# Layer 1: three regrouping transfers issued with the first mixings, a quarter of layer 0's projections added earlier, and the last group norm's small products placed two steps on

## The chip, the cores and the metric

The kernel runs on one core of a Trainium2 chip. The time is device time in microseconds of one execution; the figure before is the median of three runs. The trace is that of one profiled execution.

## The reference

Two attention layers act on x of shape (8, 512, 32, 32), each as x + layer(group_norm(x)); T = 1024 tokens, C = 512, 8 heads of 64. All is float32.

```
# layer 0
q, k, v = split(qkv_w @ norm(x))
a   = softmax(q^T k * scale) applied to v
x   = x + proj_w @ (norm(x) + a) + proj_b
# layer 1
attn = (q^T k) * scale                        # per head h
attn = einsum('gh,bhqT->bgqT', w_head, attn)  # the heads are mixed
attn = softmax(attn)
attn = (attn - mean) / sqrt(var + EPS) * gamma + beta   # over a whole head
x    = x + w_proj @ (attn @ v) + b_proj
```

## The kernel before, in words

Everything is unrolled, and the order of the instructions on each engine is the order in which the Python code issues them (a manual schedule). An Agenda is a list of functions with a slot each; `ag.run(slot)` issues those that are due, within a slot in the order in which they were added. All the transfers that this text speaks of are issued from the SP queue, but for a few small ones on POOL's. [...]

**Layer 0.** For each image the projections k, v, q and output are computed by `project0` as seven products of half-size blocks instead of eight. A result has four quarters (i, j). TensorE runs product 1, product 2 (into the same two banks of PSUM as product 1), and then products 6, 5, 7, product 3 (`banks5, left[:, 6]`, which adds to product 5's banks), and last product 4, whose two banks come from the pair tagged `a0`. VectorE adds up: `u2` from product 1 and product 6, `u3` from `u2` and product 7. `finish(i, j, x, y)` writes a quarter: for q and k two additions of 128x512 (L958), for v one of 128x1024 (L980), for the output (`out0`) one addition of 128x1024 and two of 128x512 with a store to DRAM each (L1051, L1057, L1060). Quarter (1,1) needs only `s5`, ScalarE's copy of product 5, and `u3`. The next projection's product 1 takes the `a0` banks that quarter (1,0) frees.

**Layer 1.** For each image an `Attention1` object is stepped through half-steps x = 0 to 36. Half-step x computes the scores of block x in two halves (`scores`, L1656), copies them to `raw` (L1669 on VectorE, L1671 on ScalarE), and, with a lag of MLAG = 4, mixes the heads of block y = x - 4 (`mix`, L1704), takes the exponential (L1710), and one half-step later multiplies by v (`values`, L1750). Two blocks make a step t. When the last scores of an odd x are issued, eight transfers become due for its step: each moves every eighth row of `raw` into a part of `re` (L1680, 256 KB), so that a row of `re` holds the heads side by side for the mixing. `R_ORDER` = (0, 4, 1, 5, 2, 6, 3, 7) is the order of issue and of use. `raw` has two buffers, so step t + 2 writes over step t.

When they are issued is set in three places. In the lag's first half-steps, at the end of `half_step`, `self.regroup(n=NR)` issues all that are due (NR = 8). From then on each `mix` and each `values` ends with `self.regroup(last)`, which issues one that waits for the last matmul of the call. Also, once x is above 4, each `scores` issues one piece of the next image's input (`y`, 128 KB, L1356) that waits for its own last matmul.

In the first half-steps of an image the remaining products of v (`v_pair`, L1475) fill TensorE, at slots 1 and 3. In image 0 the group norm of the eighth image's layer-0 output is also computed there, in three stages from `group_stages`: `means` (a product with `gavg`, L622, behind a VectorE copy gs_m), `squares` (four small VectorE operations and a product, L633) and `end` (some twenty small VectorE operations). `v_sums` (L1492) at slot 3 needs what `end` writes. Their products take PSUM tiles from the three buffers that scores and mixings use.

Of the kernel before, what the change touches and what calls it, by code (L numbers as in the profile page):

```python
# [467 lines left out]
def tile_two_attention_layers(  # L468
# [20 lines left out]
    B, C, T = x_d.shape  # L489
# [8 lines left out]
    NR = 8  # L498
# [198 lines left out]
    with ExitStack() as l0:  # L697
# [12 lines left out]
        def score_psum(nm):  # L710
            return ps_s.tile([P, 2, FB], F32, tag="s", name=nm)
# [174 lines left out]
        def product(banks, left, right, first, by_token):  # L886


            for i in range(2):
                for h in range(2):  # L890
                    for k in range(2):
                        if by_token:
                            out = banks[i][:, h * HC : (h + 1) * HC]
                            st, mv = right[:, k, ts(2 * i + h, P)], left[:, k]
                            start = first and k == 0 and h == 0
                        elif h == 0:
                            out = banks[i]
                            st, mv = left[:, k, ts(i, P)], right[:, k]
                            start = first and k == 0
                        else:  # L900
                            continue
                        nc.tensor.matmul(  # L902
                            out, st, mv, start=start, stop=(k == 1), skip_group_check=True
                        )

        def project0(nm, which, n, finish, by_token=False):


            left = left_t[which]
            b11, b12, b21, b22 = (n[:, 2 * i : 2 * i + 2, ts(j, FB)] for i in (0, 1) for j in (0, 1))  # L910
            s1, u2, s5 = tmp[4], tmp[5], tmp[6]

            def single(name):
                return [
                    ps_a.tile([P, FB], F32, tag="a0", name=f"{nm}_{name}_{i}", bufs=2)
                    for i in range(2)
                ]

            def double(name):
                t = score_psum(f"{nm}_{name}")  # L920
                return t, [t[:, 0], t[:, 1]]

            x = single("p1")
            product(x, left[:, 0], b11, True, by_token)
            for i in range(2):
                nc.scalar.copy(s1[:, i], x[i])
            product(x, left[:, 1], b21, False, by_token)
            finish(0, 0, x, None)
            t6, banks = double("p6")
            product(banks, left[:, 4], tmp[1], True, by_token)  # L930
            nc.vector.tensor_add(u2, s1, t6)
            t5, banks5 = double("p5")
            product(banks5, left[:, 3], tmp[0], True, by_token)
            nc.scalar.copy(s5, t5)
            t7, banks = double("p7")
            product(banks, left[:, 5], tmp[2], True, by_token)
            u3 = s1
            nc.vector.tensor_add(u3, u2, t7)
            product(banks5, left[:, 6], b22, False, by_token)
            finish(0, 1, t5, u2)  # L940
            finish(1, 1, s5, u3)
            x = single("p4")
            product(x, left[:, 2], tmp[3], True, by_token)
            finish(1, 0, x, u3)
# [256 lines left out]
        for b in range(B):  # L1201
            more = b + 1 < B
            ag = Agenda()
# [61 lines left out]
    with ExitStack() as l1:  # L1265
# [14 lines left out]
        NX = 2 * NQB * NKB  # L1280
        QLAG = NX // NQB
        R_ORDER = (0, 4, 1, 5, 2, 6, 3, 7)
        MLAG = 4
# [67 lines left out]
        def y_piece(b, i):  # L1351

            if i == 0:
                y_t[b] = shared.tile([P, NCC, T], F32, tag="n", name=f"y_{b}")
            c, r = i // 4, i % 4 * 32
            return nc.sync.dma_start(  # L1356
                out=y_t[b][r : r + 32, c], in_=x1_d[b][c * P + r : c * P + r + 32, :]
            )
# [103 lines left out]
        def k_leave():  # L1462
            for fn in due:
                fn()
            due.clear()
# [173 lines left out]
        class Attention1:  # L1639
# [237 lines left out]
            def half_step(self, x, ag):  # L1877
                y, w = x - MLAG, x - MLAG - 1
                if 0 <= w < NX:
                    self.squares(w, 0)  # L1880
                    self.sum_e(w, 0)
                if x < NX:
                    self.scores(x, 0)
                if 0 <= w < NX:
                    self.squares(w, 1)
                    self.sum_e(w, 1)
                if x < NX + MLAG:
                    k_leave()
                if 0 <= w < NX:
                    self.sum_e2(w, 0)  # L1890
                    self.sum_e2(w, 1)
                k_leave()
                if 0 <= y < NX:
                    self.mix(y, 0)
                if 0 <= w < NX:
                    self.values(w, 0)
                if x < NX:
                    self.scores(x, 1)
                if 0 <= y < NX:
                    self.mix(y, 1)  # L1900
                if x <= MLAG or x >= NX:
                    self.regroup(n=NR)
                if x >= NX:
                    self.piece(n=len(self.pieces))
                ag.run(x - 0.5)
                if 0 <= w < NX:
                    self.values(w, 1)
                    self.e.pop(w)
                    if w % QLAG == QLAG - 1:
                        qb = w // QLAG  # L1910
                        self.leave(qb)
                        self.totals(qb)
                        if qb < NQB - 1:
                            ag.at(x + 2, lambda: self.reciprocals(qb, ag, x + 2))
                            ag.at(x + 6, lambda: self.divide(qb))
                ag.run(x)
# [9 lines left out]
        for b in range(B):  # L1926
            more = b + 1 < B
            a = Attention1(b)
            ag = Agenda()
            if b == 0:  # L1930
                for x, fn in zip((0, 1, 3), group_stages(B - 1, B, small_psum1)):
                    ag.at(x, fn)
            for i in range(NV):
                ag.at(1 + 2 * i, lambda i=i: v_pair(b, NV + i))
            if b == 0:
                ag.at(3, v_sums)
            free = (NX // 2 - 2 + b) % 2
            if more:
                a.pieces += [lambda i=i: y_piece(b + 1, i) for i in range(4 * NCC)]
                a.pieces += [lambda i=i: left_piece(("k", b + 1), i) for i in range(14)]  # L1940
                for c in range(NCC):
                    ag.at(24 + c, lambda c=c: normalize1(b + 1, c))

                def k_begin():
                    kp.append(k_projection(b + 1))
                    kp[0].products(1)
                    kp[0].leave(1)

                def k_go(*ms):
                    for m in ms:  # L1950
                        kp[0].products(m)
                        due.append(lambda m=m: kp[0].leave(m))

                kp = []
                ag.at(NX - 0.5, lambda: right_tile(b + 1))
                ag.at(NX - 0.5, k_begin)
                ag.at(NX, lambda: right_y(b + 1, [0, 1]))
                ag.at(NX, lambda: k_go(2))
                ag.at(NX + 1, lambda: right_y(b + 1, [2, 3]))
                ag.at(NX + 1, lambda: k_go(6, 7))  # L1960
                ag.at(NX + 1, lambda: load_w(("v", b + 1), wvT, re_t[:, free, : NCC * C]))
                ag.at(NX + 1, lambda: left_p(b))
                ag.at(NX + 2, lambda: k_go(5, 4))
                ag.at(NX + 3, lambda: k_go(3))
            else:
                a.pieces += [lambda i=i: p_piece(i) for i in range(2 * NCC)]
            for x in range(NX + MLAG + 1):
                a.half_step(x, ag)
            if not more:
                ag.flush()  # L1970
                out1_last(a)
                continue
            a.reciprocals(NQB - 1)
            a.instance()
            ag.flush()
            v_pair(b + 1, 0)
            a.instance_end()
            a.divide(NQB - 1)
            for g in range(H):
                a.affine(g)  # L1980
            right_o = re_t[:, 1 - free].rearrange("p (i k t) -> p i k t", i=4, k=2)
            combine_right(right_o, out_view(b))
            op = out1(b, right_o)
            load_left(("q", b + 1))
            v_pair(b + 1, 1)
            load_wv_again(b + 1)
            op.run()
            q_projection(b + 1).run()
# [70 lines left out]
```

## Time and profile before

| | |
|---|---|
| median of 3 runs | 4238.78 us (4232.57 to 4243.62) |
| profiled execution | 4230.7 us |
| its span, first to last instruction | 4228.9 us |
| TensorE busy | 4152.5 us, 98% |
| VectorE, ScalarE busy | 68%, 55% |
| regrouping transfers | 1024 of 256 KB |
| mean clock of TensorE | 0.997 of full |

Layer 0 fills the span up to 1805 us, layer 1 the rest, with some 306 us an image. A line of a waits view gives the engine and what it was to run, what it waited for, and the total, the number and the longest of the waits. A line of the chain gives start, length and what ran; the chain is followed back from the last instruction, so time on it is time of the kernel. "issue" is time in which the engine waited for nothing that the profile shows. In a table of windows each engine's busy time is followed by its number of instructions, and the row ends with the granted clock, the share of time that the DMA engines were busy, and the GB/s that they moved.

### The profile page before, as it was taken

To read this page: it belongs to the slowest core of one execution; us is meant where nothing else is said; L and a number is where in the kernel's file an instruction comes from. 1 tells how busy PE (TensorE), PEld (TensorE's weight loads), DVE (VectorE), ACT (ScalarE), POOL (GpSimd) and SP (SyncE) were. 2 spreads that over 40 slices of the span, in tenths; PEclk is the share of its full clock that TensorE was granted. 3 is DMA by queue.
4 is the path that set the end of the run, shared out by engine and by line. 5 is a ranking of instruction groups with operands and counts; after the bars stand their busy time and mean duration, and the time that the engine had idled before them with its cause. 6 is when DMAs were issued, how large, how long until landed. Compare 5 with 4: busy or idle time off the path is not lost.

```text
span 4228.9 us, 131405 instructions
## 1 busy us (share of the span) xinstructions
PE 4152.5 (98%) x58572; PEld 2215.3 (52%) x58572; DVE 2861.2 (68%) x3779; ACT 2319.1 (55%) x2735; POOL 60.3 (1%) x86
## 2 busy tenths in 40 slices
PE   8999999999999999999999999999999999999998
PEld 4353535353535353456466466466466466466565
DVE  4748484848484747558668668568578588588587
ACT  2717171727272726259368278278277287286386
POOL 0000000000000000000000000000000000000000
PEclk9999999999999999999999999999999999999999
DMA  3212121212121212167467377277377376485575
GB/s 130 99 61 98 55 104 48 84 45 86 45 84 48 84 48 84 58 157 196 133 168 191 118 187 191 106 199 189 104 197 187 111 200 166 125 208 146 149 180 139
DMA packets 257905, 529.35 MB, mean 125 GB/s; under 512 B 52336, under 2 KB 59888, under 8 KB 250672
## 3 DMA queue, kind: packets, MB, share of 16 engines
q1 hardware_dynamic: 254752, 520.15, 43.1%
q8 instruction: 461, 7.55, 0.7%
q0 software_dynamic: 2576, 0.69, 0.4%
q14 instruction: 116, 0.95, 0.1%
HBM read 204.50 MB, written 46.92 MB: 59 GB/s over the span
## 4 chain that ended last, share of the span: by engine, by line
PE 92%; DVE 3%; DMA 2%; ACT 1%; issue 1%; SPq 0%; DVEq 0%; ACTq 0%
PE a L1750 12%; PE m L1704 11%; PE s L1656 11%; PE s L1082 10%; PE a L1108 10%; PE pv_p L902 5%; PE pp_p L902 5%; PE pk_p L902 5%; PE pq_p L902 4%; PE pk L1400 4%; PE pq L1400 4%; PE pv L1475 4%; PE pp L1400 3%; DMA re<-raw 1%; PE t L1781 1%
## 5 line engine op out<-in xcount | busy, mean ns | idle before, releaser
L1704 PEld LDWEIGHTS m<-wmix,re 64*64 64x64 f32 x32768 | 582.1, 135 | 120.7 <-issue 55.0
L1087 ACT ACTIVATE e<-s 128x1024 f32<-128x1024 f32 x512 | 497.2, 1026 | 234.4 <-PE s L1082 232.3
L1704 PE MATMUL m<-wmix,re 64*64 64x64 f32 x32768 | 592.2, 219 | 24.5 <-issue 17.7
L1710 ACT ACTIVATE e<-m 128x1024 f32<-128x1024 f32 x512 | 525.9, 1027 | 146.1 <-PE m L1704 142.6
L1728 DVE TENSOR_TENSOR z<-z,e 128x1024 f32<-128x1024 f32 x448 | 537.7, 1218 | 76.4 <-ACT e L1710 76.2
L1732 DVE TENSOR_TENSOR z<-z,e 128x1024 f32<-128x1024 f32 x448 | 534.1, 1219 | 62.1 <-ACT e L1721 60.4
L1750 PE MATMUL a<-e,v 128*64 128x256 f32 x4096 | 559.2, 393 | 3.1 <-issue 2.5
L1656 PE MATMUL s<-k,q 64*64 64x256 f32 x8192 | 553.6, 389 | 6.7 <-DVE q L1512 2.6
L1095 DVE TENSOR_TENSOR zacc<-zacc,e 128x1024 f32<-128x1024 f32 x384 | 468.6, 1220 | 82.6 <-ACT e L1087 61.0
L1671 ACT COPY raw<-s 128x1024 f32<-128x1024 f32 x368 | 372.9, 1013 | 267.9 <-PE s L1656 230.9
L1082 PE MATMUL s<-q,k 64*64 64x512 f32 x4096 | 490.1, 593 | 2.3 <-ACT e L1087 2.3
L1108 PE MATMUL a<-e,v 64*64 64x512 f32 x4096 | 484.1, 589 | 0.0
L1721 ACT ACTIVATE e<-e 128x1024 f32<-128x1024 f32 x448 | 460.0, 1056 | 0.0
L1656 PEld LDWEIGHTS s<-k,q 64*64 64x64 f32 x8192 | 268.3, 132 | 271.7 <-issue 167.5
L1750 PEld LDWEIGHTS a<-e,v 128*64 128x64 f32 x4096 | 251.4, 136 | 125.6 <-issue 17.3
L1108 PEld LDWEIGHTS a<-e,v 64*64 64x64 f32 x4096 | 156.7, 133 | 282.8 <-issue 282.5
L1082 PEld LDWEIGHTS s<-q,k 64*64 64x64 f32 x4096 | 147.9, 133 | 275.2 <-issue 241.4
L1669 DVE COPY raw<-s 128x1024 f32<-128x1024 f32 x144 | 175.9, 1221 | 97.4 <-PE s L1656 89.0
L1475 PE MATMUL pv<-wv,y 128*128 128x512 f32 x256 | 116.3, 608 | 0.3 <-DVE raw L1669 0.3
L1480 DVE COPY v<-pv 128x512 f32<-128x512 f32 x30 | 20.7, 689 | 139.3 <-ACT v L1479 139.3
L902 PE MATMUL pv_p<-left_v,tmp 128*128 128x256 f32 x512 | 113.1, 379 | 0.0
L902 PE MATMUL pq_p<-tmp,left_q 128*128 128x512 f32 x256 | 112.5, 592 | 0.0
(316 smaller groups left out, 4128.3 us busy)
## 6 DMA issues: line engine op xcount, KB each, us to landing
re<-raw SPq DMA_DIRECT2D x1024, 256.0 KB
rzb<-zd SPq DMA_DIRECT2D x256, 128.0 KB
left_q<-left_q SPq DMA_DIRECT2D x17, 1792.0 KB
left_p<-left_p SPq DMA_DIRECT2D x17, 1792.0 KB
left_k<-left_k SPq DMA_DIRECT2D x10, 1792.0 KB
x<-in_x_dram SPq DMA_DIRECT2D x32, 512.0 KB
x<-x SPq DMA_DIRECT2D x64, 256.0 KB
left_v<-left_v SPq DMA_DIRECT2D x8, 1792.0 KB
```

Of the source, the lines that this page charges most:

```text
L902: nc.tensor.matmul(out, st, mv, start=start, stop=(k == 1), skip_group_check=True)
L1082: nc.tensor.matmul(ps[c * D : c * D + D, m], k[r, hp, k0 : k0 + D], q[r, hp, ts(f, FB)], start=True, stop=True,)
L1087: nc.scalar.activation(e[i], ps, AF.Exp, scale=S0 * S0)
L1095: nc.vector.tensor_add(zacc[g], zacc[g], e[i])
L1108: nc.tensor.matmul(acc[g][a][m * D : m * D + D], v[rows, kc, ts(2 * hp + m, D)], e[i][rows, m], start=(kc == 0), stop=(kc == NG - 1),)
L1400: nc.tensor.matmul(self.ps[m][:, i], w[:, left, k * HC + i * P : k * HC + i * P + P], right[:, k], start=(k == 0 and m != 2), stop=(k == 1 ...
L1656: last = nc.tensor.matmul(pv[c * D : c * D + D, m, j], qo_t[b][r, 2 * qb + j, hp, ts(c, D)], k_t[b][r, hp, ts(kb, KB)], start=True, stop=True,
L1704: last = nc.tensor.matmul(ps[c * D : c * D + D, a, ts(r, D)], self.re[t, r][rows, j, k0 : k0 + D], wmix[rows].rearrange("p g i -> p (g i)" ...
L1710: nc.scalar.activation(self.e[y][:, j], ps.rearrange("p a c -> p (a c)"), AF.Exp)
L1728: nc.vector.tensor_add(self.z[:, j], self.z[:, j], self.e[y][:, j])
L1732: nc.vector.tensor_add(self.z2[:, j], self.z2[:, j], self.e2[j])
L1750: last = nc.tensor.matmul(self.acc[w][two * D : two * D + D, s].rearrange("p (c i) -> p c i", i=Q8), v_t[b][:, kc, ts(g, D)], e[:, g], sta ...
```

## The change

There are three edits. In `project0` the quarter (1,1) is finished right after `u3`, ahead of product 3, where before it was finished after quarter (0,1). In `half_step` the call at the end of x = 3 issues five of its eight transfers, and the call at x = 4 is gone; the three that are left are issued one by one by the calls in `mix`. In image 0 of layer 1, `means` moves from slot 0 to slot 1 and `squares` from slot 1 to slot 2, `means` behind `v_pair`; `end` stays first in slot 3.

```
@@ project0
             nc.vector.tensor_add(u3, u2, t7)
+            finish(1, 1, s5, u3)
             product(banks5, left[:, 6], b22, False, by_token)
             finish(0, 1, t5, u2)
-            finish(1, 1, s5, u3)
             x = single("p4")
@@ half_step
-                if x <= MLAG or x >= NX:
-                    self.regroup(n=NR)
+                if x < MLAG or x >= NX:
+
+                    self.regroup(n=NR if x != MLAG - 1 else 5)
@@ the loop over images of layer 1
+            stages = group_stages(B - 1, B, small_psum1) if b == 0 else ()
             if b == 0:
-                for x, fn in zip((0, 1, 3), group_stages(B - 1, B, small_psum1)):
-                    ag.at(x, fn)
+                ag.at(3, stages[2])
             for i in range(NV):
                 ag.at(1 + 2 * i, lambda i=i: v_pair(b, NV + i))
             if b == 0:
+                ag.at(1, stages[0])
+                ag.at(2, stages[1])
                 ag.at(3, v_sums)
```

## The prediction

> **What bounds the kernel now.** I read the page first: TensorE is busy 98% of the span, so the time can fall only where TensorE idles or runs at a reduced clock. Of the 76 us of idle time, some 20 lie ahead of its first projection and 10 after its last output product. What is left is small pieces, so the next views are the list of who TensorE waited for in layer 1 (first fence; columns: us in total, times, longest) and the chain that ended last, stretch by stretch.
>
> ```profile
> PE m L1704 <- issue: 17.1, 23, 2.5
> PE m L1704 <- DMA re<-raw: 4.4, 8, 1.6
> PE s L1656 <- issue: 2.2, 1, 2.2
> ```
>
> The largest line waits for nothing that the profile names ("issue"): 17 us. In the chain the longest of these stand at one place of an image, just after its first mixing. In image 1:
>
> ```profile
> 2148.22 0.87 PE s L1656 x16
> 2149.08 0.57 PE m L1704 x37
> 2149.65 1.21 issue
> 2150.86 0.68 PE m L1704 x27
> ```
>
> Images 1 to 6 lose 1.21, 2.45, 1.11, 2.24, 0.91 and 1.50 us there, images 0 and 7 none. What TensorE lacks is instructions. Counting its instructions in order, nearly every longer "issue" gap of layer 1 sits at one position modulo 256, and ends 1.3 to 1.6 us after a packet of the instruction queue q8 lands. The DMA view says when that packet could run: ahead of image 2's stall, over 8.0 us, the data queue alone fills the engines and no instruction packet appears; it comes in the next stretch.
>
> ```profile
> q1 hardware_dynamic: 1103, 2.03, 104.3%
> re<-raw SPq DMA_DIRECT2D x6, 256.0 KB
> ...
> q1 hardware_dynamic: 36, 0.05, 14.1%
> q8 instruction: 1, 0.02, 5.3%
> ```
>
> (The first two lines are 2448.5 to 2456.5, the last two 2456.5 to 2458.) That queue holds the eight regrouping transfers of step 1, issued together when x = 3 ends. Two of the stalls cost more than their length: the stretches right after them run at half clock (last but two value of a row):
>
> ```profile
> 1811.30:1818.10 6.80, 6.14 (x24) 2.61 (x17) 1.68 (x5) 1.01 (x1) 0.00 (x0) 0.50 0.47 118
> 2459.80:2463.20 3.40, 3.40 (x80) 3.15 (x74) 1.82 (x2) 3.15 (x4) 0.00 (x0) 0.50 0.14 43
> 3077.60:3081.00 3.40, 3.40 (x70) 2.27 (x61) 2.43 (x3) 1.02 (x1) 0.00 (x0) 0.50 0.18 43
> ```
>
> The first row follows the wait of the last group norm, the other two the 2.45 and 2.24 us stalls; stalls of 1.6 us and less have no such stretch.
>
> [...]
>
> **The change, part by part.**
>
> *Regrouping.* At x = 3 five transfers go out in place of eight; the other three follow mix(0,0), mix(0,1) and mix(1,0), one each, by the regroup call that mix already makes. The count stays 1024. In image 1 the eight move from about 2139.4 to 2148.0, 1.04 us each, so five drain 3.1 us earlier, near 2145. The relief is bounded by when the block is asked for. Once TensorE enters the block before, an undisturbed fetch of layer 1 begins some 0.8 us later (0.6 to 1.2 are common); the six begin 1.8, 2.5, 1.3, 2.5, 1.0 and 2.3 us later. The gains are 1.0, 1.7, 0.5, 1.7, 0.2 and 1.5 us; images 3 and 5 ask so late (24.5 to 24.8 us after their first score) that the first deferred transfer, released at 24.0, can be in the way, so I count nothing for them: 5.9 us. The two stalls above 2.2 us fall below 1, so their half-clock stretches go: 2 x 3.41 x 0.5 = 3.4 us. Part sum **9.3 us**; bounds: all six stalls and both stretches, 12.8, and below nothing, as the second rival shows. On the SP queue the three wait for the end of a mixing, with two y pieces and step 2's transfers behind them; those wait for later matmuls anyway, and the engines carry little from 2149 to 2154 (DMA share 0.11). The last one's reader, the end of mix(2,0), comes 6.2 us after its release; the buffer for raw of step 3 is wanted at the same time.
>
> *The quarter.* VectorE now adds quarter (1,1) while TensorE is in product 3, not after quarter (0,1), so it reaches the last quarter, whose banks the next product needs, earlier. Worked on the chain at 500:
>
> ```profile
> 497.47 0.02 DVEq L958
> 497.49 0.04 issue
> 497.54 3.40 DVE q L958 x5
> 500.94 0.04 issue
> 500.98 3.27 PE pp_p L902 x7
> ```
>
> Product 4 starts at 497.26 and has eight matmuls 0.43 apart, so the next could start at 500.70: 0.28 us lost, at seven q-to-output hand-overs 2.0 us. The k-to-v hand-over of the first image loses 0.29 the same way. In the seven later ones a 0.64 us sum of exponentials stands between and the wait is for the second bank, which ends with product 4 itself: nothing. v to q shows no gap. Once, at 1735, the permuted q of layer 1 has six additions of 1.0 us and k starts at 1741.85; with the (1,1) pair done by 1735.6 the last addition starts when its bank is ready at 1739.2 and k at 1740.3: 1.55 us. Part sum **3.8 us**, 3 to 4.5. The moved quarter costs nothing where product 3 covers it: 2.4 to 3.3 us with the addition before, against 3.43; the output's is 3.9, so quarter (0,1) starts 0.4 us later there, and its bank is still free 1.6 us before a score wants it. The stores of the output change order on SP and leave earlier.
>
> *Last group norm, once.* Before, TensorE stands 2.36 us for gs_m and 0.66 for gs_sq (the rows pm L622 and pv L633 in the waits) and v_pair's product starts at 1813.65. After, scores of x = 1 follow at once, one waiting some 0.9 us for ScalarE's raw copy, and that product starts near 1810.1: 3.55 us gained. But gs_m now stands behind v_pair's copy on VectorE (0.59 + 0.69 us and hand-overs), so TensorE waits about 1.5 us for pm, then 1.3 for gs_sq behind a 1.23 us raw copy; the next v_pair starts 7.3 us after the first one's end instead of 5.1: 2.2 lost. Net 1.35. The 6.83 us at half clock go or stay (0 to 3.4); I take half, 1.7. Part sum **3.0 us**, bounds -2 (both new waits trigger half clock) and 5.
>
> The sum is 9.3 + 3.8 + 3.0 = 16.1 us. The profiled execution took 4230.7 us (span 4228.9 and 1.8 around it), so it would take 4214.6; the median of the runs shown is 8.1 us above it, and taken from that the forecast is **4222.7 us**, 0.38% faster.
>
> **Rivals.** *The fetch isn't freed.* The block may be asked for late, not held back, since the late starts are 1 to 2.5 us [...]. Then only 3.8 + 3.0 remain: 4232.0. For it: images 3 and 5. Against it: in all six images the packet starts 25.5 to 25.8 us after the first score, though their block boundaries differ by 1.8 us; what they share is the moment that the data queue drains.
>
> *The deferred transfer is late (slower).* In the chain a regrouping transfer takes 4.78 to 6.66 us from release to use. The last deferred one has 6.2. If it queues behind the two before it and the y piece and takes 8.5, mix(2,0) stands 2.3 us and the clock halves for 1.7 more: 4.0 x 8 images = 32 us, less the 16.1: 4254.7. It is slower by 0.3% from about 8.1 us on. Against it: the steady steps release their last transfer 5 us ahead with fuller engines and mostly lose under 1 us.
>
> That the change doesn't do what it says is excluded: the instruction order on SP shows the three transfers among the y pieces.
>
> **How the numbers follow.** A difference under 0.3% (12.7 us) can't be told from none. The main case has 0.70: its spread of 10 to 24 us puts 0.55 above the bound and 0.15 within. The first rival has 0.20 (0.03 faster, 0.17 same), the second 0.10 (0.08 slower, 0.02 same). Faster 0.58, same 0.34, slower 0.08. The range reaches from all stalls and both first and last clocks gained (22 us) with the 5 us by which runs scatter on one side, to the second rival's beginning on the other: 4210 to 4238.
>
> **What the profile after would show.** Right: the first 30 us of images 1, 2, 4 and 6 without an issue gap over 1 us, no half-clock stretch near 2460 and 3078, an instruction packet 23 to 25 us after the first score; product 4 followed at once by the output projection; pm and gs_sq waits of 1 to 1.5 us. Wrong: issue gaps as long as before, or a row of m waiting for re<-raw at the third mixing of each image.

## The result, and the profile after

| | before | after |
|---|---|---|
| median, first timing (5 runs each) | 4239.43 us (4232.57 to 4243.62) | 4217.70 us (4217.51 to 4219.02) |
| ratio, first timing | | 0.995 (0.9939 to 0.9962) |
| median, second timing (30 and 5 runs) | 4231.94 us (4225.59 to 4239.96) | 4217.72 us (4214.50 to 4223.78) |
| ratio, second timing | | 0.9967 (0.9954 to 0.9980) |
| profiled execution, span | 4228.9 us | 4215.8 us |
| TensorE busy, idle | 4152.5, 76.4 us | 4147.3, 68.5 us |

The kernel became faster, by 0.3 to 0.5%: 21.7 us in the first timing, 14.2 us when it was timed again. The difference between the two is all in the kernel before (4239 and 4232 us); the changed kernel has 4217.7 both times. The spans of the two profiled executions differ by 13.1 us: 7.9 us less idle time of TensorE and 5.2 us less busy time. Before, 20.5 us in five stretches ran at half clock, after 3.4 us in one (without a stretch at the very end, 6.5 and 7.2 us).

Who TensorE waited for in layer 1, after:

```profile
PE m L1704 <- issue: 14.0, 28, 1.1
PE m L1704 <- DMA re<-raw: 5.7, 10, 1.3
PE a L1750 <- issue: 1.0, 4, 0.3
```

The total of "issue" before mixings fell only from 17.1 to 14.0 us, but the longest from 2.5 to 1.1; the line of scores with its single 2.2 us wait is gone, and that before the products with v fell from 2.5 to 1.0. The chain shows the place that matters, image 2 after its first mixing. Before:

```profile
2455.99 0.91 PE m L1704 x59
2456.90 2.45 issue
2459.35 0.28 PE m L1704 x3
```

After, scores and mixings follow each other there:

```profile
2447.12 1.02 PE s L1656 x16
2448.15 0.93 PE m L1704 x64
2449.08 0.87 PE s L1656 x16
2449.95 0.96 PE m L1704 x64
```

The DMA view of the same image, first 2440.5 to 2447.5, then 2448 to 2450:

```profile
re<-raw SPq DMA_DIRECT2D x5, 256.0 KB
...
q8 instruction: 1, 0.02, 3.0%
...
re<-raw SPq DMA_DIRECT2D x1, 256.0 KB
```

Five transfers instead of eight, and the instruction packet has the engines almost to itself: no line of q1 in the second stretch (beside q8's 3.0% there is one packet of q14, 1.7%), though the first deferred transfer is issued there. The packet starts 23.2 us after the image's first score, where it was 25.5.

Granted clock (last but two value of a row) in the counterparts of the three half-clock stretches of before, with the one stretch that is left in image 0 as the second row (it stands right behind the 128 small products of `v_sums`; more on that below):

```profile
1805.00:1811.80 6.80, 6.80 (x24) 2.96 (x16) 0.79 (x1) 1.01 (x1) 0.00 (x0) 1.00 0.61 153
1831.50:1834.90 3.40, 3.40 (x84) 2.75 (x80) 0.00 (x0) 1.55 (x2) 0.00 (x0) 0.51 0.03 5
2453.00:2456.40 3.40, 3.40 (x96) 2.31 (x92) 1.87 (x3) 3.40 (x4) 0.00 (x0) 1.00 0.65 183
3066.00:3069.40 3.40, 3.40 (x94) 2.26 (x90) 1.75 (x2) 3.06 (x4) 0.00 (x0) 1.00 0.57 157
```

The quarter's move, in the chain at the hand-over from q to output, where 3.40 us of VectorE stood between the products:

```profile
491.83 7.72 PE pq_p L902 x18
499.55 3.86 PE pp_p L902 x9
```

VectorE is off the chain there. At the hand-over from q to k of layer 1 two additions ended the wait before:

```profile
1739.75 2.06 DVE q L1018 x2
1741.81 0.04 issue
1741.85 3.27 PE pk_p L902 x7
```

After, one is left:

```profile
1735.87 1.09 DVE q L1018
1736.96 0.04 issue
1737.00 5.42 PE pk_p L902 x12
```

The waits of TensorE in the first part of image 0, before (1800 to 1830 us):

```profile
PE pm L622 <- DVE gs_m L620: 2.4, 1, 2.4
...
PE pv L633 <- DVE gs_sq L631: 0.7, 1, 0.7
```

After (1795 to 1850 us):

```profile
PE pm L622 <- DVE gs_m L620: 1.6, 1, 1.6
...
PE pv L633 <- DVE gs_sq L631: 1.2, 1, 1.2
PE s L1656 <- ACT raw L1671: 0.9, 1, 0.9
...
```

The three of after are the waits that the prediction named for the new order (about 1.5, 1.3 and 0.9 us).

### The profile page after: what moved, and what is told of

Same layout as the page of the kernel before. It is cut to its first block, busy times and chain, and to the rows that moved or that the text cites. A ratio compares the mean times of both kernels' runs of the same rounds, so it can differ in the third digit from the quotient of the medians.

```text
span 4215.8 us, 131422 instructions
## 1 busy us (share of the span) xinstructions
PE 4147.3 (98%) x58572; PEld 2216.2 (53%) x58572; DVE 2868.0 (68%) x3779; ACT 2318.4 (55%) x2735; POOL 60.3 (1%) x86
## 4 chain that ended last, share of the span: by engine, by line
PE 93%; DMA 2%; DVE 2%; ACT 1%; issue 1%; SPq 0%; DVEq 0%; ACTq 0%
PE a L1750 12%; PE m L1704 12%; PE s L1656 11%; PE s L1082 10%; PE a L1108 10%; PE pk_p L902 5%; PE pq_p L902 5%; PE pv_p L902 5%; PE pp_p L902 5%; PE pk L1400 4%; PE pq L1400 4%; PE pv L1475 4%; PE pp L1400 3%; PE t L1781 1%; DMA re<-raw 1%
## 5 line engine op out<-in xcount | busy, mean ns | idle before, releaser
L1093 DVE TENSOR_TENSOR zacc<-e,e 128x1024 f32<-128x1024 f32 x64 | 78.3, 1223 | 53.6 <-ACT e L1087 53.6
```

## The experiments

Two theories stood at the start. **A**: the batch of regrouping transfers holds back TensorE's instruction packet until the data queue has drained. **B**: the block is asked for late, and the batch has no part in it. **C** is the late deferred transfer. In the trace of before all 19 "issue" gaps of layer 1 over 0.5 us stand at position 193 or 194 of 256 in the count of TensorE's instructions, weight loads among them, and end 1.31 to 1.63 us after a packet of q8 has landed:

```profile
PE 4152.5 (98%) x58572; PEld 2215.3 (52%) x58572; DVE 2861.2 (68%) x3779; ACT 2319.1 (55%) x2735; POOL 60.3 (1%) x86
...
q8 instruction: 461, 7.55, 0.7%
```

That is one packet of 16 KB for 254 matmuls and weight loads. The 256 instructions from one such position to the next are called a block here, and the time at which TensorE enters the block before is called the request. That a packet is asked for just then is the author's estimate, from packets that start 0.2 to 0.8 us after it in images 1 to 7 of after. What tells A from B is one number per image, the "issue" gap between 24 and 32 us after the image's first score. Here it is for every kernel (us, from the traces; in brackets the transfers in the batch; a dash is under 0.3):

| kernel | im. 1 | 2 | 3 | 4 | 5 | 6 | 7 |
|---|---|---|---|---|---|---|---|
| before (8 in the batch) | 1.21 | 2.45 | 1.11 | 2.24 | 0.91 | 1.50 | - |
| after (5) | - | - | - | - | 0.97 | - | - |
| after, second profile | - | 0.33 | - | - | 0.91 | 0.42 | - |
| regrouping edit alone (5) | - | - | - | - | - | 0.43 | - |
| quarter alone (8) | 1.07 | 1.63 | 1.11 | 2.24 | 0.63 | 1.41 | - |
| group norm alone (8) | 1.01 | 1.66 | 1.15 | 1.16 | 0.91 | 1.52 | - |
| before, 12 | 2.25 | 1.56 | 3.03 | 2.36 | 2.83 | 2.79 | 1.71 |
| after, 5 and 3 again | 1.12 | 1.67 | 1.15 | 1.32 | 0.91 | 1.71 | - |
| after, 6 | - | 0.56 | - | - | - | 0.31 | - |
| after, 4 | - | - | - | - | 0.63 | 0.38 | - |
| before, blocks 36 later | 0.91 | 1.70 | 0.32 | 1.36 | - | 1.65 | - |
| before, blocks 112 earlier | 1.62 | 1.23 | 1.78 | 0.90 | 1.64 | - | 1.60 |
| after, blocks 112 earlier | - | - | 0.75 | 0.66 | 0.42 | - | 0.51 |

In the rows with four to six in the batch, the gaps of image 6, and in the last row those of images 3, 5 and 7, lie at 30.6 to 31.4 us, before the next block and not the one behind the first mixing.

**The parts alone.** Each of the three edits was put into the kernel before by itself.

The regrouping edit:

```
-                if x <= MLAG or x >= NX:
-                    self.regroup(n=NR)
+                if x < MLAG or x >= NX:
+                    self.regroup(n=NR if x != MLAG - 1 else 5)
```

> Only the regrouping edit. Theory A (the batch of eight holds back TensorE's instruction packet): the issue gaps after the first mixing of images 1, 2, 3, 4 and 6 are gone or under 0.3 us, image 5 keeps about 1 us, no half-clock stretch near 2460 and 3078, while those near 1811 and 4177 stay. Gain 9 to 10 us in the profiled execution (5.9 us of stalls, 3.4 us of half clock, and image 3's 1.1 us). If the stalls are also what makes the times of the kernel before scatter over 11 us, the five times lie within 4 us of each other, and the gain of the median is larger, up to 15 us. Rival B (the block is asked for late, and the batch has no part in it): the stalls stay, gain under 2 us, scatter as before.

Measured: 4225.68 us median of 18 runs against 4232.81 us of 47, ratio 0.998 (0.9973 to 0.9987), which is 8.5 us with an interval of 5.5 to 11.4 (the medians differ by 7.1). The gaps went from 9.4 us in the trace of before to 0.4, and no half-clock stretch follows an image's first mixing. What TensorE still waits for instructions in layer 1:

```profile
PE m L1704 <- issue: 10.3, 20, 1.3
```

Rival B is out. One expectation failed: the runs still lie 10 us apart (4219.25 to 4229.37), so these stalls are not what makes the times scatter.

The quarter:

```
             nc.vector.tensor_add(u3, u2, t7)
+            finish(1, 1, s5, u3)
             product(banks5, left[:, 6], b22, False, by_token)
             finish(0, 1, t5, u2)
-            finish(1, 1, s5, u3)
```

> Only quarter (1,1) ahead of product 3. By the prediction's sum 3.8 us (eight gaps of 0.28 us and 1.55 us at the hand-over from q to k of layer 1), so a profiled gain of 3 to 4.5 us. The stalls of images 1 to 6 and both half-clock stretches after them stay under theory A, and the five times scatter by some 10 us as those of the kernel before do; so the median is uncertain by that much. Rival (the scatter has its cause elsewhere, at the projections): the times lie within 3 us of each other.

Measured: 4227.57 us (21 runs), ratio 0.9992 (0.9985 to 0.9998), 3.4 us (5.2 between the medians). The traces are sharper: the time from TensorE's 500th matmul to the first score is 1679.3 to 1679.9 us in the runs without the edit that have no half clock in between, and 1675.1 to 1676.4 us in the six with it: about 4 us. Each of the seven hand-overs from q to output is 0.29 us shorter (24.03 us from the first product of q to that of the output, 24.32 before), and the one from q to k of layer 1 by 1.56 (25.47 for 27.03). The stalls stay, as theory A says.

The group norm:

```
-                for x, fn in zip((0, 1, 3), group_stages(B - 1, B, small_psum1)):
-                    ag.at(x, fn)
+                ag.at(3, stages[2])
...
+                ag.at(1, stages[0])
+                ag.at(2, stages[1])
```

> Only the last group norm's products moved. By the prediction's sum 1.35 us of waits, and 1.7 us if half of the clock loss near 1811 goes, 3.4 if all of it goes: since the trace of the changed kernel shows no half clock there, 4.7 us now, 3 to 5.5. Waits for raw, gs_m and gs_sq of about 0.9, 1.6 and 1.2 us in image 0 as in the changed kernel. The stalls of images 1 to 6 stay, and the times scatter by some 10 us. Rival (the half clock near 1811 went because of the quarter's move, which shortens the wait at 1735 to 1742 before it): the stretch stays here and the gain is 1.3 us.

Measured: 4230.89 us (14 runs), ratio 0.9992 (0.9984 to 1.0000), 3.4 us with an interval that reaches to nothing (1.9 between the medians). The new waits are there (0.93, 1.57, 1.24 us). No half clock near 1811, but 6.8 us of it at 1834; and the runs with the regrouping or the quarter alone, which have the old group norm, have none at 1811 either. That stretch belonged to one execution and proves nothing for this edit.

The three ratios sum to 0.36%, 15.3 us, and the three differences of medians to 14.3; the whole change was timed again beside them:

> The changed kernel once more, on the chip of the three runs above and with many runs of the kernel before beside it. If the difference on record (21.7 us) holds some luck of the five runs of the kernel before, the difference is here nearer the sum of the three parts run alone, 15 us (8.5 + 3.4 + 3.4). If the parts help each other, it stays above 20 us.

Measured: 4217.72 us, ratio 0.9967 (0.9954 to 0.9980), 14.0 us. The parts add up within the noise. The 21.7 us of the first timing hold some 7 us that five runs of the kernel before happened to be slower; whether that was chance or the chip they ran on is open.

**More and fewer in the batch.** Four transfers issued twice in the kernel before:

```
                 if x <= MLAG or x >= NX:
                     self.regroup(n=NR)
+                if x == MLAG - 1:
+                    for r in R_ORDER[:4]:
+                        nc.sync.dma_start(out=self.re[1, r], in_=self.raw[1][r::NR])
```

> The kernel before, with four of the eight transfers of the second step issued once more at the end of x = 3 (same source, same target): twelve in the batch, and their readers wait for nothing longer, since step 1 is read some 12 us later. Theory A: the data queue drains about 4.2 us later, at 29.7 us after the first score of an image, so the packet that landed at 25.5 to 25.8 us comes at about 29.7 us and every stall after the first mixing of images 1 to 6 grows by about 4 us, and stalls appear in images 0 and 7 where a block boundary falls into the window: 6 to 8 x 4 us and half-clock stretches after each, 25 to 50 us slower, about 4265 to 4290 us. Rival B (asked for late): stalls and time as before, within 5 us; the DMA engines have room. Rival C (the mixings would wait for their operands, not for instructions): the gaps are put down to re<-raw, at the third mixing.

Measured: 4246.51 us (6 runs), ratio 1.0038 (1.0023 to 1.0052): 16 us slower, between the two theories. The stalls grew in five of the six images and one appeared in image 7, but none grew by the 4 us that draining would cost, and that of image 2 is shorter than before. The chain and the DMA view of image 3 show why. The chain:

```profile
2761.70 0.86 PE s L1656 x16
2762.57 0.73 PE m L1704 x49
2763.30 3.03 issue
2766.33 0.70 PE m L1704 x15
```

The data and instruction queues in 2760.5 to 2763.7 (first line) and in 2763.7 to 2764.5:

```profile
q1 hardware_dynamic: 445, 0.81, 107.0%
...
q1 hardware_dynamic: 102, 0.19, 101.1%
q8 instruction: 1, 0.02, 10.0%
```

The instruction packet runs in the middle of a data queue that is still full. The first score of this image is at 2735.91 us and the packet starts 27.9 us later, while q1 is at 101%. So A in its first form is wrong: the packet isn't held until the queue drains. Counted from the request, it starts after 0.2 to 0.8 us where five were queued and have left (images 1 to 7 of after), after 1.0 to 2.5 us where eight were queued (images 1 to 6 of before), and after 1.7 to 3.4 us with twelve; its starts with twelve lie about one transfer (1.04 us) apart: 24.7, 25.8, 26.6 and 27.8 us after the first score. That is the time of one to three transfers, and in no image here of more. Which of the queued transfers it waits for, the traces don't show.

The changed kernel with the batch made eight long again, the three deferred ones still deferred:

```
                     self.regroup(n=NR if x != MLAG - 1 else 5)
+                if x == MLAG - 1:
+                    for r in R_ORDER[:3]:
+                        nc.sync.dma_start(out=self.re[1, r], in_=self.raw[1][r::NR])
```

> The changed kernel, with three of its five transfers at the end of x = 3 issued once more (same source, same target): the batch is eight long again, and the other three are still deferred to the first mixings. Theory A (the length of the batch holds the instruction packet back): the stalls after the first mixing of images 1 to 6 come back, 1 to 2.5 us each, 9 to 10 us together, with one or two half-clock stretches: 8 to 14 us slower than the changed kernel. As twelve transfers held the packet for two or three transfers and not to the end of the batch, no delay should be above 3.4 us after the block before is entered. Rival D (the gain comes from the deferral itself, a transfer moved out of a busy time): stalls stay away, the time is within 2 us of the changed kernel.

Measured: 4224.46 us (22 runs), 6.7 us above the changed kernel's median, ratio to before 0.9981 (0.9975 to 0.9988). All six stalls are back, 7.9 us together; in image 2, in the chain:

```profile
2450.00 0.64 PE m L1704 x40
2450.64 1.67 issue
```

So the length of the batch does it, not the deferral. The loss is smaller than the 8 to 14 us expected: in images 2 and 4 the packet started at 24.8 us, 0.7 and 0.9 us earlier than in the trace of before, and no half clock followed a stall after a first mixing.

Four and six in place of five:

```
-                    self.regroup(n=NR if x != MLAG - 1 else 5)
+                    self.regroup(n=NR if x != MLAG - 1 else 4)   # and 6
```

> The changed kernel with four transfers at the end of x = 3 and four deferred; the fourth goes after the first product with v, 4.8 us ahead of its use at the third mixing (5.8 us for the third in the changed kernel). Theory A: the batch drains before any block of images 1 to 7 is asked for already with five, so nothing more is gained: within 2 us of the changed kernel. Rival C (the deferred transfer is late): it takes more than 4.8 us from release to use, and the third mixing of each image waits for re<-raw by up to 1.9 us: up to 15 us slower.

> The changed kernel with six transfers at the end of x = 3 and two deferred. Theory A: the batch drains 1.04 us later, at 23.7 us after the first score; blocks asked for at 23.0 to 23.4 us (images 2, 4 and 6) are held 0.3 to 0.7 us, those asked for later (1, 3, 5, 7) are not: stalls of under 0.7 us in those three images, 1 to 2 us slower than the changed kernel. Under rival B (asked for late) there is no such grading.

Measured: four, 4220.18 us (8 runs), ratio 0.9973 (0.9963 to 0.9983); six, 4216.71 us (5 runs), ratio 0.9965 (0.9952 to 0.9978). Neither can be told from five (0.9967). With four no mixing waits for `re` between 24 and 40 us after the first score of any image: 4.8 us from release to use were enough there, and rival C is out with room to spare. With six the grading that was expected isn't shown. At the block behind the first mixing, image 2 has 0.56 us, image 4 has 0.23 and image 6 nothing, while the second profile of the changed kernel, with five, has 0.33 in image 2 too. The chain of image 2 with six:

```profile
2446.65 0.91 PE m L1704 x58
2447.56 0.56 issue
```

**Moving the blocks.** If, as theory A has it, a stall is set by where a block ends while transfers are queued, moving all the blocks must move the stalls to other images. Products that nobody reads were put ahead of layer 1:

```
         load_wv_again(0)
+        more = small_psum1("more")
+        for _ in range(55):
+            nc.tensor.matmul(more[:, :32], ones, ones[:, :32], start=True, stop=True)
```

> The kernel before, with 55 small products whose result nothing reads (ones times 32 columns of ones, two instructions each) on TensorE ahead of layer 1: every block of 256 instructions then ends 110 instructions earlier in the schedule, and nothing else moves; they cost some 5 us once. Theory A: a stall is set by where the block ends while the batch is in the queue. From the instruction counts of the changed kernel's trace, blocks are asked for at 23.0, 24.7, 23.2, 24.9, 23.4, 25.0 and 23.6 us after the first score in images 1 to 7, and needed at 25.5, 27.2, 25.9, 27.8, 26.5, 28.6 and 26.7; with a packet at 24.8 to 25.8 us and 2.75 us from its start to work, the stalls after the first mixing become 1.7 to 2.6, 1.1, 1.5 to 2.4, 0.7, 1.5, 0 and 1.4 us, where they were 1.21, 2.45, 1.11, 2.24, 0.91, 1.50 and 0: images 1, 3, 5 and 7 gain a longer one, 2, 4 and 6 a shorter one. Rival B2 (each image has its own cause, such as its data or its place in the run): images 2, 4 and 6 keep the long ones.

Measured: each product became four instructions, not two (110 matmuls and 110 weight loads for 55), so the blocks moved by 220, which is 36 later, and the expectation was for another shift. What it showed still fits: the requests come 0.2 to 0.9 us later than before in images 1 to 7, and five of the six stalls are shorter, that of image 3 by 0.8 us and that of image 5 gone; image 6 kept its stall (1.65 us). Only images 3 and 5 tell, since images 2 and 4 have stalls that short in the trace of the group norm alone as well, where no block moved. The time was 4242.67 us, against 4235.92 of the kernel before beside it (one run each); the extra products themselves cost more than that, so only the gaps are read. Again with 28 products:

> The kernel before with 28 of the extra products ahead of layer 1. The trace of the run with 55 showed four instructions for each (its TensorE matmuls rose by 110 and its weight loads by 110), so blocks there ended 220 instructions earlier, which is 36 later modulo 256; 28 make 112 earlier, what that run was to do. Theory A: blocks are asked for at 23.0, 24.7, 23.2, 24.9, 23.4, 25.0 and 23.5 us after the first score in images 1 to 7 and needed at 25.5, 27.2, 25.9, 27.7, 26.5, 28.6 and 26.7. With packets at 24.8 to 25.8 us and 2.75 us from a packet's start to work, stalls after the first mixing of 1.7 to 2.6, 1.1, 1.5 to 2.4, 0.7, 1.5, 0 and 1.4 us: long in images 1, 3, 5, 7, short in 2, 4, 6, the reverse of the kernel before. Rival B2 (each image has its own cause): 2, 4 and 6 keep the long ones.

Measured: 1.62, 1.23, 1.78, 0.90, 1.64, 0 and 1.60 us, against 1.7 to 2.6, 1.1, 1.5 to 2.4, 0.7, 1.5, 0 and 1.4. Images 1, 3, 5 and 7 now have the long stalls, 2, 4 and 6 the short ones. Image 3, in the chain:

```profile
2779.81 0.63 PE s L1656 x9
2780.44 1.78 issue
2782.22 0.44 PE s L1656 x4
```

It stands among scores now, at another instruction, with nothing changed but the count. And the changed kernel with the same 28:

> The changed kernel with the same 28 extra products, which put its blocks at the places of the run above. Theory A: five transfers have left the queue at 22.7 us, before any block is asked for (23.0 us and later), so no image has a stall over 1 us after its first mixing, wherever its blocks end. Rival (the five suit only the places that the blocks happened to have): stalls of 1.5 us and more in images 1, 3, 5 or 7.

Measured: no gap above 0.75 us. With five in the batch the stalls stayed away with the blocks at either place. The times of these two, one run each, were 4248.50 and 4228.90 us, against 4233.65 of the kernel before.

## Why the prediction was right

The time fell, to within the range, and the largest part came from where the prediction put it: with a shorter batch the instruction packet starts earlier and the stalls after the first mixing go. Part by part it is less even.

**Base.** Forecast 4222.7 us, measured 4217.7. The forecast took 16.1 us from the median of the three runs. Against 30 runs of the kernel before the change was worth 14.2 us, 1.9 less than forecast, and against five 21.7. The median of the 30 is 6.8 us under that of the three, so the 5 us of miss come from the base, and the error of the parts took a little off it. The profiled execution of before (4230.7 us) already lay near the 4232 us of the later timings.

**Regrouping, 9.3 us forecast, 8.5 (5.5 to 11.4) measured alone.** The step that read the packets of the six as late ("the six begin 1.8, 2.5, 1.3, 2.5, 1.0 and 2.3 us later") against some 0.8 us when undisturbed was right. Three terms were mis-sized. The undisturbed delay is 0.2 to 0.8 us in the trace of after, so the stalls of images 1, 2, 4 and 6 went entirely, where 0.2 to 0.75 us was left for three of them. Image 3, counted as nothing, gained its 1.1 us. Image 5 kept 0.97 us for the reason given: its packet took 1.8 us, against a median of 1.05 us in that trace, beside the first deferred transfer (in its trace q1 takes 54% of the engines and q8 5% from 3367.6 to 3370 us). The other way, the 3.4 us of half clock were read off one execution: the same code has one such stretch in the trace of the quarter alone and none in that of the group norm alone, where images 2 or 4 stall by one transfer (0.8 to 1.1 us) less. A part of the stalls and of the clock was luck of the profile.

The reason was partly wrong: "what they share is the moment that the data queue drains" fitted eight transfers, but with twelve the packet started at most 3.4 us after the request. In image 3 with twelve the request came at 2760.4 us, and over the next 3.2 us q1 moved 445 packets of the trace (0.81 MB, some three transfers) and q8 none; then the one instruction packet got in while q1 was at 101%. What sets the order of the two queues, no run here shows.

**Quarter, 3.8 us forecast, 3.4 timed and about 4 in the traces.** Right in its two large terms, 2.0 and 1.55 us forecast and 2.0 and 1.56 found. The 0.29 us of the first image's hand-over from k to v can't be told from the scatter there (26.4 to 27.1 us). One thing wasn't counted: the wait from q to k of layer 1 was followed by 3.4 us at half clock in two of the six traces without this edit and in none of the seven with it.

**Group norm, 3.0 us forecast, 3.4 (0 to 6.8) timed.** The sum fits a timing that can't tell it from nothing; its terms don't hold. The step that failed is the net 1.35 us of waits. Old order, in the traces of the regrouping, the quarter and the twelve transfers: waits of 2.36, 1.23, 0.38 and 0.25 us, 4.2 together. New order: 0.93, 1.57, 1.23 and 0.48, again 4.2. From the first score to the first mixing of image 0, with half of the half-clock time taken off, it is 31.8 to 31.9 us in these three and 31.4 to 31.5 in the six with the edit: 0.4 us gained. The prediction read the old gs_sq wait as 0.66 us; that was a half-clock execution (0.50 from 1811.28 to 1818.11 us), in which slower products filled the rest of the time. The clock term, 1.7 us, isn't shown. It was meant for the 6.83 us at half clock near 1811 us, and of the four traces with the old order and no extra products only that of before has them; the six with the new order have none there. The other half-clock time of image 0 stands elsewhere: in ten of the thirteen traces, with both orders, a stretch begins while the 128 products of `v_sums` (L1492, 128x8, some 4 us) run, or at most 0.7 us after them. The stretch at 1834 us in the run of the group norm alone is one of these.

**The rivals.** That the fetch isn't freed is refuted by the batch sizes. That the deferred transfer is late is refuted by four in the batch. For that rival the prediction read 4.78 us as the shortest time of a regrouping transfer in the chain; the chain of before has one of 4.35 us, at 3245.69.

**Given back.** The stalls (8.4 us less), the quarter (3.8) and the clock should have gained more than 13.1 us in the profile. Outside the place after the first mixing, waits for instructions in layer 1 rose from 12.4 to 13.7 us and for `re` from 4.4 to 5.7. Transfers follow each other steadily there, and in the middle of the cases the packet starts 1.3 (before) and 1.4 us (after) after the request. The sum of these waits for instructions differs from execution to execution: with eight in the batch it is 16.6 us for the quarter alone and 14.8 for the group norm alone, with five 12.7 for the regrouping alone and 17.0 in the second profile of the changed kernel. So a price of the change isn't shown there, and the rest of the difference stays open.

## What to carry to other kernels

When an engine waits for nothing that the profile names, count its instructions. In before all 19 such gaps of layer 1 over 0.5 us stood at one position modulo 256 and ended 1.31 to 1.63 us after an instruction packet had landed, and what made the difference was which transfers were queued when the block before began: 9.4 us of stalls in the table above with eight in the batch, 0.4 with five (the regrouping edit alone). The batch stood where TensorE used up its blocks fastest: behind the first mixing a block of 256 lasted 2.5 to 3.7 us in images 1 to 7 of after, against some 4.5 us on average in the steady part of an image. Here three transfers of 128 in an image, issued a little later, were worth about as much as the other two edits together. A stretch of half clock in one profile can be a draw: the one near 1811 us is in one of the four traces with the old order and no extra products. Price it from several executions.

## What was not expected of the hardware

With twelve transfers in the batch an instruction packet started up to 3.4 us after the request, the time of some three transfers of 256 KB at 1.04 us each, and in image 3 it ran while q1 was at 101% of the engines.

No one length of idle time separates the stalls that half clock followed from the others. In the run with twelve transfers a stall of 1.71 us in image 7 was followed by half clock, and one of 2.79 us in image 6 was not; the stretches of 3.4 us after them (3698.7 and 4008.3 us):

```profile
3698.70:3702.10 3.40, 3.40 (x114) 2.55 (x117) 1.17 (x1) 1.19 (x2) 0.00 (x0) 1.00 0.31 71
4008.30:4011.70 3.40, 3.40 (x79) 3.10 (x78) 0.26 (x1) 1.01 (x1) 0.00 (x0) 0.50 0.09 20
```

What the traces show besides is where the idle time falls. In each trace with several slow stretches their starts lie whole multiples of 3.413 us apart, to within 5 ns (in before 1811.28, 1838.59, 2459.81, 3077.63 and 4176.72 us). The thirteen traces were cut into windows of that length, from 30 to 4190 us, and those that themselves ran at half clock left out. Ten windows have TensorE busy for less than 1.46 us, and every one of these is followed by half clock. Of the fifteen with 1.46 to 1.83 us four are. Of the rest only one is (2.06 us), apart from windows full of small products. The stall of 1.71 us lay inside one window; that of 2.79 us was split between two, so neither had more than some 1.8 us of idle time. The windows ahead, first that of the 1.71 us stall, then the one in which most of the 2.79 us fell:

```profile
4004.87:4008.28 3.41, 1.71 (x33) 0.87 (x26) 2.18 (x3) 2.44 (x3) 0.00 (x0) 1.00 0.96 224
3694.28:3697.70 3.42, 1.61 (x65) 1.22 (x56) 2.52 (x3) 3.42 (x4) 0.00 (x0) 1.00 1.07 251
```

They are two of the fifteen, the first followed by half clock and the second not, so busy time alone doesn't decide it. The idle time that half clock always followed in these windows is shorter than a window: 3.41 us less the 1.46 us of busy time, some 2 us.

TensorE also ran at half clock while busy. The 110 products of 32 columns in a row (55 extra products) ran with no idle time between records and at half clock (0.51):

```profile
1807.00:1827.00 20.00, 20.00 (x106) 19.40 (x109) 0.29 (x2) 0.00 (x0) 0.00 (x0) 0.51 0.00 1
```

They took 21.0 us in the chain instead of the 5 us expected. In the kernels themselves the 128 small products of `v_sums` stand at such stretches: in after they ran from 1827.29 to 1831.12 us, and the clock was 0.50 from 1831.55 to 1834.96.
